# A two-layer kernel: one store per tile of values with its surroundings copied within DRAM, early loads moved behind C's rows, and attention's pools waiting tile by tile

## The chip, the cores and the metric

The kernel runs on one core of a Trainium2 chip. The core has five engines that work side by side, each through its own list of instructions in order: TensorE (PE), VectorE (DVE), ScalarE (ACT), GpSimd (POOL) and SyncE (SP), which here issues nearly all DMAs. The metric is the device time of the core in microseconds (us), the median of three runs. Engines wait for each other through semaphores; an instruction that waits holds back all that stands behind it on its engine, the issuing of DMAs included.

## The reference, cut to what matters

Input x is 4 images of 384 channels and 64 x 64 points. Each of two layers normalises x by groups and adds its output to x.

```python
# layer 0: a selective state-space layer over the L = 4096 points of an image
xz = einsum('blc,dc->bld', layernorm(gn(x)), in_proj_w)      # 384 -> 2 x 768
xb, z = split(xz)
xc = silu(causal_conv4(xb) + conv_b)
dt, B, C = split(xc @ x_proj_w.T)                             # 24, 16, 16
dt = softplus(dt @ dt_w.T + dt_b)
h_t = exp(dt_t * A) * h_{t-1} + (dt_t * xc_t) * B_t           # 768 x 16 states, along L
y = (sum over states of h_t * C_t + xc * D) * silu(z)
x = x + y @ out_proj_w.T
# layer 1: attention of each point over a window of 7 x 7 around it, 12 heads of 32
q, k, v = split(w_qkv @ gn(x));  k, v padded by 3 at each side with their edge values
attn = softmax(q * scale . k in the window + rel_bias)
x = x + w_proj @ (sum over the window of attn * v) + b_proj
```

Everything is float32. The change concerns the padded v, which both parts of the kernel hand to each other through DRAM.

## The kernel before, in words

**State-space layer** (`state_space_layer`, from line 366). The points of the four images are cut into 44 chunks of 372 or 376, eleven per image. A chunk is worked in 24 steps: 6 blocks of 128 channels by 4 groups of 4 states. For each step the drive dt*x*B is made by POOL or DVE (`drive`, line 908; the list `DRIVES`, line 109, says which), DVE runs four scans, POOL multiplies the states by C (`times_c`, line 952), PE sums them by transposing into a PSUM bank (`sums`, 966). B and C come as rows out of DRAM, spread over 128 partitions (`load_bc`, 781), eight buffers of 744 KB for both together. Ahead of the scans a chunk needs its projections: `load_w` (691) brings twelve pieces of the input projection's weights in turn into three buffers, `in_proj` (695) multiplies, `x_proj` (762) makes dt, B and C, and `x_rows` (772) copies them with ACT and stores B's and C's rows (bcrows).

All of this, for all chunks, is put into one list with a tick each (`put`, line 507; the ticks stand in the table `AT`, line 43, 16 ticks to a step, 384 to a chunk), sorted once by tick (line 1178) and written down in that order. `Written` (line 144) makes the instructions of each engine keep the written order. All instructions are made inside one helper, so the profile shows all of them as line 154. SP's list is thus the order of ticks too: a DMA that waits holds back the DMAs with later ticks, though SP runs ahead of the engines where nothing makes it wait. Each DMA signals one of eight semaphores in turn, and it is not issued before the DMA that used that semaphore last has landed.

From chunk 13 on, the layer also prepares attention for images already done: three tiles of 128 points per chunk of values (`value_load`, `value_mm`, `value_out`, `value_store`; the three stores have ticks 631, 263 and 458, that is 247 in the next chunk, 263, and 74 in the next chunk), and a tile of keys and one of queries. 88 tiles of values, 22 of the 32 stripes of attention, are made here. A tile k covers rows 2k and 2k+1 of the image.

`store_values` (line 323) writes a tile into `vdr`, the padded array of 70 x 70 points. It issues one DMA of 64 x 384 elements for each row, and for each side one of 3 x 384 that repeats the row's first or last point: six DMAs. The tile with an image's first or last row writes that row four times: fifteen DMAs. At tick 263 of one chunk comes the last tile of image 0 or 1, at tick 247 the first tile of image 0, 1 or 2; the third image's last rows are made in attention. Right behind the store at 247 (-137 seen from the next chunk) stands the load of a piece of w_in at tick -128, for the `in_proj` at -122.

**The hand-over.** `begin_attention` (line 1145) stands one tick after the last `in_proj`. It closes the pool of the projections' buffers, makes stripe 0's keys `kt`, queries `q` and the table `bias` in their place, and issues their six loads at once. In SP's list this is ahead of the last chunk's loads of B's last rows (tick 20) and of C's rows (21, 22, 62).

**Attention** (`attention_layer`, line 1181). 32 stripes of eight image rows; a stripe is 12 units (4 pairs of blocks of 8 x 8 points by 3 groups of 4 heads). The loop at line 1457 writes in each iteration parts of several units: `divide` (DVE, POOL), `scores` (PE, then DVE adds bias and takes the maximum, ACT the exponential), `turn` (PE transposes), `weigh` (PE, with the values `vw`), and projections for stripes ahead (`pieces`, 1350). `load_pair_values` (357) loads values of a pair as four DMAs of 98 x 384; `load_keys` (1272) loads keys and queries of a stripe. While the iteration number is negative these are issued by ACT, later by SP. `surround` (1277) copies a stripe's border keys between neighbours on POOL. Stripes 22 to 31 compute their values here (`value`, 1243), with the same `store_values`.

The attention pools are opened (line 1187) in the memory of the state-space layer's pools. Opened without `reuse_waits="tile"`, the first use of such memory waits for everything that used the old pools.

Of the kernel before, what the change touches and what calls it, by code (L numbers as in the profile page):

```python
# [15 lines left out]
C = 384  # L16
NJ = C // P
HW = 64
# [15 lines left out]
STEP = 16  # L34
CHUNK = STEP * STEPS
# [135 lines left out]
def two_layers(  # L171
# [150 lines left out]

    def store_values(dq, b, k, v):

        for row in range(2):
            y = 2 * k + row
            to = [PAD + y]
            if y == 0:
                to += range(PAD)
            if y == HW - 1:  # L330
                to += range(PAD + HW, HP)
            a = row * HW
            for t in to:
                dq.dma_start(vdr[b][t, PAD : PAD + HW, :], v[a : a + HW, :])
                for c, p in ((0, a), (PAD + HW, a + HW - 1)):
                    dq.dma_start(
                        vdr[b][t : t + 1, c : c + PAD, :],
                        v[p : p + 1, :].unsqueeze(1).broadcast_to([1, PAD, C]),
                    )

    def load_stripe_keys(dq, kt, s):
        b, r = s // NXT, s % NXT
        for m in range(NJ):
            dq.dma_start(
                kt[:, m, PAD : PAD + RB, PAD : PAD + HW],
                kdr[b][m * P : (m + 1) * P, r * TX : (r + 1) * TX].rearrange(
                    "p (r c) -> p r c", r=RB
                ),
            )

    def load_stripe_queries(dq, q, s):
        b, r = s // NXT, s % NXT
        dq.dma_start(
            q, qdr[b][:, r * TX : (r + 1) * TX].rearrange("(k p) t -> p k t", p=P)
        )
# [10 lines left out]
    def state_space_layer(eng):  # L366
# [5 lines left out]
        with ExitStack() as es:  # L372
# [134 lines left out]
            def put(tick, fn, *args):  # L507
                score.append((tick, len(score), fn, args))
# [588 lines left out]
                )  # L1097


            tiles = [(b, k) for b in range(NB - 1) for k in range(L // P)]  # L1100
            for X in range(len(chunks)):
                for i in range(len(AT["value_mm"])):
                    if not tiles or X < NCHUNK * (tiles[0][0] + 1) + 2:
                        break
                    b, k = tiles[0]
                    left = (len(chunks) - X) * len(AT["value_mm"]) - i
                    if k % NPAIR == 0 and left < NPAIR:
                        break
                    cell = {"at": tiles.pop(0)}
                    have_values.add((b, k))  # L1110
                    for name, fn in (
                        ("value_load", value_load), ("value_norm", value_norm),
                        ("value_mm", value_mm), ("value_out", value_out),
                        ("value_store", value_store),
                    ):
                        put(CHUNK * X + AT[name][i], fn, cell)


            turns = sorted(range(2 * NJ), key=lambda n: AT["key_mm"][n])
# [25 lines left out]
            def begin_attention():  # L1145
                preps.close()
                home = ctx.enter_context(
                    tc.tile_pool(name="early", bufs=1, reuse_waits="tile", side="right")
                )
                kt = home.tile([P, NJ, RW, HP], F32, name="kt0")  # L1150
                q = home.tile([P, NJ, TX], F32, name="q0")
                bias = early["bias"] = home.tile([P, NH, NK], F32, name="bias")
                early["kt"], early["q"] = [kt], [q]
                load_stripe_keys(dq, kt, 0)
                load_stripe_queries(dq, q, 0)
                for e in range(2):
                    dq.dma_start(bias[e * QB : (e + 1) * QB].rearrange("p h k -> p (h k)"), bm)

            put(
                CHUNK * (len(chunks) - 1) + 1 + max(  # L1160
                    max(AT[name]) for name in ("in_proj", "in_bias", "conv", "x_rows", "dt_mm")
                ),
                begin_attention,
            )


            put(-120, dq.dma_start, w_out, out_wT.rearrange("(k p) m -> p k m", p=P))
# [13 lines left out]
    def attention_layer(eng, gm1, qkb, pjb, early, mv):  # L1181
# [2 lines left out]
        stripes = NB * NXT  # L1184
        with ExitStack() as es:
            def pool(name, **kw):
                return es.enter_context(tc.tile_pool(name=name, **kw))

            wt = pool("wt1", bufs=1)
            w_qkv = wt.tile([P, NJ, 3 * C], F32, name="w_qkv")  # L1190
# [21 lines left out]
            def of(s):  # L1212
                return s // NXT, s % NXT
# [5 lines left out]
            def kt_of(s):  # L1219
                return ring([P, NJ, RW, HP], "kt", 4, s)  # L1220
# [7 lines left out]
            def vw_of(k):  # L1228
                return ring([P, 2, NCH, C], "vw", 3, k)
# [39 lines left out]
                )  # L1269
                surround(s, m)  # L1270

            def load_keys(s, dq):
                if s > 0:
                    load_stripe_keys(dq, kt_of(s), s)
                    load_stripe_queries(dq, q_of(s), s)

            def surround(s, m):

                b, r = of(s)
                kt = kt_of(s)  # L1280
                own = kt[:, m, PAD : PAD + RB, :]
                for c, e in ((0, PAD), (PAD + HW, PAD + HW - 1)):
                    ge.tensor_copy(
                        own[:, :, c : c + PAD], own[:, :, e : e + 1].broadcast_to([P, RB, PAD])
                    )
                if r > 0:
                    ge.tensor_copy(kt_of(s - 1)[:, m, PAD + RB :, :], own[:, 0:PAD, :])
                else:
                    ge.tensor_copy(kt[:, m, 0:PAD, :], own[:, 0:1, :].broadcast_to([P, PAD, HP]))
                if r < NXT - 1:  # L1290
                    ge.tensor_copy(kt_of(s + 1)[:, m, 0:PAD, :], own[:, RB - PAD :, :])
                else:
                    ge.tensor_copy(
                        kt[:, m, PAD + RB :, :], own[:, RB - 1 : RB, :].broadcast_to([P, PAD, HP])
                    )
# [46 lines left out]
            def has_values(s):  # L1342
                b, r = of(s)
                return (b, NPAIR * r) in have_values

            def has_keys(s):
                b, r = of(s)
                return (b, 2 * r) in have_keys and (b, 2 * r + 1) in have_keys
# [108 lines left out]
            for s in range(-3 * UNITS, N + 12):  # L1457
                stripe, k = s // UNITS, s % UNITS
                for f in waiting:
                    next(f, None)  # L1460
                waiting = []
                if s == 4:
                    output_bias(mm)
                if s > 4 and last_stats:
                    last_stats.pop(0)()
                if 0 <= s - 4 < N and (s - 4) % NJ == NJ - 1:
                    keep(s - 4)
                if 0 <= s - 1 < N:
                    divide(s - 1)
                if 0 <= s < N:  # L1470
                    scores(s)
                if 0 <= s - 2 < N:
                    turn(s - 2)
                mine = pieces(stripe, k)
                for n, (f, t, i) in enumerate(mine):
                    ps = mm if s >= 0 else (mm, *lgs)[(s + n) % 5]
                    if n == 1 and 0 <= s - 3 < N:
                        weigh(s - 3)
                    g = f(t, i, ps)
                    next(g)  # L1480
                    if n < len(mine) - 1:
                        next(g, None)
                    else:
                        waiting.append(g)
                if len(mine) < 2 and 0 <= s - 3 < N:
                    weigh(s - 3)
                if k == 0 and 0 <= stripe - 1 < stripes:
                    load_res(stripe - 1)
                if 0 <= stripe + 2 < stripes and has_keys(stripe + 2):
                    if k == 0:  # L1490
                        load_keys(stripe + 2, se if s < 0 else dq)
                    if k in (4, 6, 8):
                        surround(stripe + 2, (k - 4) // 2)
                if k == 2 and 0 <= stripe + 3 < stripes and not has_keys(stripe + 3):
                    load_x(stripe + 3)
                if s == 3 - UNITS:
                    dq.dma_start(w_pj, proj_wT.rearrange("(k p) m -> p k m", p=P))
                if s == 2 * UNITS:
                    dq.dma_start(w_qkv, qkv_wT.rearrange("(k p) m -> p k m", p=P))
                if 6 <= k < 6 + NJ and 0 <= stripe + 3 < stripes and not has_keys(stripe + 3):  # L1500
                    gn(stripe + 3, k - 6)
                pair = (s + 1) // NJ + 1
                if (s + 1) % NJ == 0 and 0 <= pair < stripes * NPAIR:
                    load_pair_values(se if s < 0 else dq, vw_of(pair), pair)

    engines = [
        Written(tc, e) for e in (nc.tensor, nc.vector, nc.scalar, nc.gpsimd, nc.sync)
# [49 lines left out]
```

## Time and profile before

| | us |
|---|---|
| median of three runs | 6690.64 (6688.14 to 6691.85) |
| the profiled execution's own time | 6691.2 |
| its span | 6689.4 |
| PE busy (matmul) in the span | 6224.9 |
| DVE, ACT, POOL busy | 5838.8, 5612.8, 5676.5 |
| last scan of the state-space layer ends | about 5158.5 |
| last statistics of the state-space layer end | 5182.2 |
| attention's first exponential starts | 5203.03 |

The page cuts the span into 40 slices of 167 us and gives each engine's busy tenths. A group row has the engine, the operation, output and inputs, the shapes, the number of instructions, then busy us and mean ns, then the idle time just ahead of the group and what ended most of it. In a timeline a row is a start, a duration, the instruction and how many of its kind follow one another; [5.91 <-ACT state] means that the engine had been idle for 5.91 us, and that an instruction of ACT on state ended that. SPq and ACTq rows are DMAs that SP or ACT issues, with the time its sequencer spent on them. A row of the windows view has a stretch, its length, then busy us and number of instructions of PE, PE's weight loads, DVE, ACT and POOL, the clock granted to PE, the mean busy share of the 16 DMA engines, and GB/s.

The time between two stores of bcrows is the length of a chunk. It is 112.6 us in chunks 38 to 42 and 113.5 in most of chunks 16 to 33; it is 119.28, 118.11, 120.52, 117.44 and 118.87 in the chunks that end at 1806, 2836, 3072, 4100 and 4335.

### The profile page before, as it was taken

Reading aid. Unit: us, or ns where it says so; the run is one execution under the profiler, and the core shown is the slowest. Engines: PE = TensorE matmul, PEld = TensorE weight load, DVE = VectorE, ACT = ScalarE, POOL = GpSimd, SP = SyncE. Lnnn points to the kernel's source line nnn. Section 1 sums busy time; section 2 is a strip of 40 time slices with the busy share of each in tenths; the row PEclk is TensorE's granted clock in tenths of the full one; section 3 lists DMA queues with packets and bytes.
Section 4 is the critical chain, followed back from the end, with each engine's and each line's share of the span. In section 5 each row is a group of like instructions: output and inputs, shape, how many; then the busy total and the mean of one; then the engine's idle time right before and its main releaser. Section 6 shows DMA issues by size and latency. Waiting matters only on the chain.

```text
span 6689.4 us, 134599 instructions
## 1 busy us (share of the span) xinstructions
PE 6224.9 (93%) x47526; PEld 4275.4 (64%) x47526; DVE 5838.8 (87%) x10102; ACT 5612.8 (84%) x14147; POOL 5676.5 (85%) x3032
## 2 busy tenths in 40 slices
PE   6888888989999999999999999999996899999999
PEld 4666666666666676666666666676765555555555
DVE  4999999999999999999999999999998666555555
ACT  4888888888999999999999999999995778665556
POOL 3999999999999999999999999999998555444443
PEclk9999999999999999999999999999998999999999
DMA  5242323232444445353535344453532555223332
GB/s 186 88 132 90 132 91 129 87 135 93 159 138 147 150 127 162 123 165 119 176 118 162 123 149 136 125 157 121 159 121 79 153 159 157 97 97 106 100 103 92
DMA packets 790234, 860.06 MB, mean 129 GB/s; under 512 B 200344, under 2 KB 710072, under 8 KB 789432
## 3 DMA queue, kind: packets, MB, share of 16 engines
q1 hardware_dynamic: 785200, 848.68, 40.2%
q8 instruction: 377, 6.18, 0.4%
q10 hardware_dynamic: 4360, 2.78, 0.2%
q14 instruction: 297, 2.43, 0.1%
HBM read 740.60 MB, written 110.81 MB: 127 GB/s over the span
## 4 chain that ended last, share of the span: by engine, by line
DVE 33%; PE 29%; ACT 26%; issue 6%; POOL 4%; DMA 1%; SPq 1%; POOLq 0%; DVEq 0%; ACTq 0%
DVE h L154 29%; PE mm L154 17%; ACT da L154 9%; PE pt L154 4%; POOL h L154 4%; PE yps L154 4%; ACT L154 3%; ACT sg L154 3%; PE ov L154 2%; PE lg L154 2%; ACT dt L154 2%; ACT sz L154 2%; DVE xn L154 1%; ACT xD L154 1%; ACT pT L154 1%
## 5 line engine op out<-in xcount | busy, mean ns | idle before, releaser
L154 DVE TENSOR_TENSOR_SCAN h<-da,h 128x373 f32<-128x373 f32 (+1 forms) x4224 | 3616.6, 913 | 88.4 <-ACT da L154 74.5
L154 POOL TENSOR_TENSOR h<-h,BC 128x1488 f32<-128x1488 f32 (+1 forms) x1056 | 3257.7, 3102 | 68.4 <-ACT state L154 65.2
L154 ACT ACTIVATE da<-dt,nega 128x372 f32<-128x372 f32 (+1 forms) x4224 | 2378.6, 571 | 313.7 <-DVE h L154 279.8
L154 POOL TENSOR_TENSOR h<-dtx,BC 128x372 f32<-128x372 f32 (+6 forms) x1056 | 1754.6, 1682 | 52.8 <-ACT dtx L154 35.8
L154 PE MATMUL yps<-ident,h 128*124 128x128 f32 (+1 forms) x12672 | 1603.7, 279 | 138.7 <-POOL h L154 136.7
L154 PEld LDWEIGHTS yps<-ident,h 128*124 128x124 f32 (+1 forms) x12672 | 1457.0, 142 | 352.5 <-POOL h L154 226.6
L154 PE MATMUL mm<-xn,w_in 128*128 128x372 f32 (+3 forms) x3168 | 1099.0, 487 | 84.0 <-DMA w_in<-wdr 40.5
L154 POOL TENSOR_TENSOR sg<-sg,rs 128x784 f32<-128x784 f32 x384 | 574.0, 1495 | 643.2 <-DVE rs L154 490.2
L154 ACT ACTIVATE sg<-sg,mx 128x196 f32<-128x196 f32 x1536 | 685.1, 448 | 404.6 <-DVE mx L154 359.7
L154 DVE TENSOR_TENSOR h<-dtxps,BC 128x1488 f32<-128x1488 f32 (+6 forms) x792 | 967.6, 1235 | 2.1 <-ACT dtx L154 1.4
L154 PEld LDWEIGHTS mm<-xn,w_in 128*128 128x128 f32 x3168 | 576.6, 192 | 417.6 <-DVE h L154 56.6
L154 PE MATMUL mm<-xb,cw 128*128 128x372 f32 (+1 forms) x2112 | 699.5, 477 | 23.9 <-ACT xc L154 18.2
L154 DVE CUSTOM_DVE_ANT_0 sg<-lg,bias 128x196 f32<-128x196 f32 x1536 | 464.3, 358 | 186.0 <-PE lg L154 177.9
L154 PEld LDWEIGHTS mm<-xb,cw 128*128 128x128 f32 x2112 | 393.8, 189 | 285.3 <-ACT xc L154 35.5
L154 ACT ACT_TABLE_LOAD x441 | 565.8, 1283 | 8.7 <-PEq L1542 0.8
L154 PE MATMUL mm<-yg,w_out 128*128 128x372 f32 (+1 forms) x1584 | 526.1, 478 | 0.0
L154 PE MATMUL pt<-ident,sg 128*98 128x128 f32 x3072 | 446.6, 281 | 29.0 <-ACT pT L154 21.4
L154 PEld LDWEIGHTS pt<-ident,sg 128*98 128x98 f32 x3072 | 313.7, 128 | 181.6 <-issue 78.7
L154 PEld LDWEIGHTS mm<-yg,w_out 128*128 128x128 f32 x1584 | 288.7, 191 | 152.9 <-issue 1.6
L154 PEld LDWEIGHTS ov<-pT,vw 98*32 98x32 f32 x12288 | 189.6, 110 | 193.3 <-issue 136.7
L154 ACT ACTIVATION_READ_ACCUMULATOR sg<-sg,mx 128x1 f32 x1536 | 287.8, 187 | 0.0
L154 PE MATMUL mm<-xp,w_qkv 128*128 128x512 f32 x612 | 279.5, 593 | 0.0
(136 smaller groups left out, 7106.3 us busy)
## 6 DMA issues: line engine op xcount, KB each, us to landing
BC<-bcrows SPq DMA_DIRECT2D x320, 744.0 KB
w_in<-wdr SPq DMA_DIRECT2D x528, 192.0 KB
vw<-vdr SPq DMA_DIRECT2D x504, 147.0 KB
cw<-ddr SPq DMA_DIRECT2D x264, 256.0 KB
xs<-in_x_dram SPq DMA_DIRECT2D x210, 186.0 KB
wk<-in_qkv_wT_dram SPq DMA_DIRECT2D x180, 192.0 KB
o<-x SPq DMA_DIRECT2D x96, 256.0 KB
out_dram<-o SPq DMA_DIRECT2D x96, 256.0 KB
```

Source lines behind the costliest of these rows:

```text
L154: ins = made(*args, **kw)
```

## The change

- A tile of values is stored by one DMA of 2 x 64 x 384 elements. The surroundings are made by a new function, `pad_values`, once per stripe: for each side one DMA from `vdr` to `vdr` that repeats the first or last column of eight rows three times, and for the first and last stripe of an image one that repeats a whole row of 70 points three times. In the state-space layer these stand 24, 48 and 72 ticks after the stripe's last store; in attention at units 6, 7 and 8 of the stripe two ahead of use.
- `begin_attention` stands behind the last C row (tick 62) too. Its loads follow one by one, 32 ticks apart: kt, q, and bias in two halves.
- All pools of attention are opened with `reuse_waits="tile"`: a tile waits for the last users of the tiles that lay in its memory.
- Before attention's first unit, ACT issues only the three loads of keys of stripe 1; that stripe's queries and the first two pairs of values are issued by SP.

PE's, DVE's and POOL's lists are otherwise the same instructions in the same order; ACT's lacks nine DMAs; SP's has 2633 rows in place of 3001.

```diff
     def store_values(dq, b, k, v):
-        for row in range(2):
-            y = 2 * k + row
-            to = [PAD + y]
-            if y == 0:
-                to += range(PAD)
-            if y == HW - 1:
-                to += range(PAD + HW, HP)
-            a = row * HW
-            for t in to:
-                dq.dma_start(vdr[b][t, PAD : PAD + HW, :], v[a : a + HW, :])
-                for c, p in ((0, a), (PAD + HW, a + HW - 1)):
-                    dq.dma_start(
-                        vdr[b][t : t + 1, c : c + PAD, :],
-                        v[p : p + 1, :].unsqueeze(1).broadcast_to([1, PAD, C]),
-                    )
+        dq.dma_start(vdr[b][PAD + 2 * k : PAD + 2 * k + 2, PAD : PAD + HW, :], v)
+
+    def pad_values(dq, b, r, side):
+        rows = vdr[b][PAD + RB * r : PAD + RB * (r + 1)]
+        if side < 2:
+            c, e = ((0, PAD), (PAD + HW, PAD + HW - 1))[side]
+            dq.dma_start(
+                rows[:, c : c + PAD, :], rows[:, e : e + 1, :].broadcast_to([RB, PAD, C])
+            )
+        elif r in (0, NXT - 1):
+            y, e = (0, PAD) if r == 0 else (PAD + HW, PAD + HW - 1)
+            dq.dma_start(
+                vdr[b][y : y + PAD], vdr[b][e : e + 1].broadcast_to([PAD, HP, C])
+            )
...
+                    stored[b, k // NPAIR] = max(
+                        stored.get((b, k // NPAIR), 0), CHUNK * X + AT["value_store"][i]
+                    )
+            for (b, r), tick in stored.items():
+                for side in range(3):
+                    put(tick + 24 * (side + 1), pad_values, dq, b, r, side)
...
                 early["kt"], early["q"] = [kt], [q]
-                load_stripe_keys(dq, kt, 0)
-                load_stripe_queries(dq, q, 0)
-                for e in range(2):
-                    dq.dma_start(bias[e * QB : (e + 1) * QB].rearrange("p h k -> p (h k)"), bm)
...
+            tick = CHUNK * (len(chunks) - 1) + 1 + max(
+                max(AT[name])
+                for name in ("in_proj", "in_bias", "conv", "x_rows", "dt_mm", "load_c")
+            )
+            put(tick, begin_attention)
+            for n in range(4):
+                put(tick + 2 * STEP * (n + 1), early_load, n)
...
-                return es.enter_context(tc.tile_pool(name=name, **kw))
+                return es.enter_context(tc.tile_pool(name=name, reuse_waits="tile", **kw))
...
-            def load_keys(s, dq):
+            def load_keys(s, key_queue):
                 if s > 0:
-                    load_stripe_keys(dq, kt_of(s), s)
+                    load_stripe_keys(key_queue, kt_of(s), s)
                     load_stripe_queries(dq, q_of(s), s)
...
+                t = stripe + 2
+                if 0 <= t < stripes and not has_values(t) and k in (6, 7, 8):
+                    pad_values(dq, *of(t), k - 6)
...
-                    load_pair_values(se if s < 0 else dq, vw_of(pair), pair)
+                    load_pair_values(dq, vw_of(pair), pair)
```

More of the change, by code (lines that the diff above doesn't have):

```diff
@@ L1097, in state_space_layer @@
                 )
+            stored = {}
             tiles = [(b, k) for b in range(NB - 1) for k in range(L // P)]
@@ L1153, in begin_attention, with early_load @@
                 early["kt"], early["q"] = [kt], [q]
-                load_stripe_keys(dq, kt, 0)
-                load_stripe_queries(dq, q, 0)
-                for e in range(2):
-                    dq.dma_start(bias[e * QB : (e + 1) * QB].rearrange("p h k -> p (h k)"), bm)
[L1159 to L1163, printed above, removed]
-            )
+            def early_load(n):
+                if n == 0:
+                    load_stripe_keys(dq, early["kt"][0], 0)
+                elif n == 1:
+                    load_stripe_queries(dq, early["q"][0], 0)
+                else:
+                    e = n - 2
+                    dq.dma_start(
+                        early["bias"][e * QB : (e + 1) * QB].rearrange("p h k -> p (h k)"), bm
+                    )
+            tick = CHUNK * (len(chunks) - 1) + 1 + max(
+                max(AT[name])
+                for name in ("in_proj", "in_bias", "conv", "x_rows", "dt_mm", "load_c")
+            )
+            put(tick, begin_attention)
+            for n in range(4):
+                put(tick + 2 * STEP * (n + 1), early_load, n)
             put(-120, dq.dma_start, w_out, out_wT.rearrange("(k p) m -> p k m", p=P))
```

## The prediction

> **What bounds the kernel now.** I read the page's engine shares and slices first, then the groups, then the timelines of POOL, SP, PE and ACT around every place where POOL idles. Slices 1 to 30 are the state-space layer, in which the slice rows give four engines 8 to 9 tenths; the rest is attention, in which PE alone has 9.
>
> ```profile
> PE   6888888989999999999999999999996899999999
> POOL 3999999999999999999999999999998555444443
> L154 POOL TENSOR_TENSOR h<-h,BC 128x1488 f32<-128x1488 f32 (+1 forms) x1056 | 3257.7, 3102 | 68.4 <-ACT state L154 65.2
> L154 POOL TENSOR_TENSOR h<-dtx,BC 128x372 f32<-128x372 f32 (+6 forms) x1056 | 1754.6, 1682 | 52.8 <-ACT dtx L154 35.8
> ```
>
> The two POOL groups make (3257.7 + 1754.6)/44 = 113.9 us of work per chunk, and bcrows issues follow one another by 112.6 to 113.5 us in most chunks: POOL sets the pace, and an interval longer than that is one in which POOL idled. Its timeline shows where. The first case, SP beside PE and POOL, in the chunk that stores the first tile of image 0:
>
> ```profile
> 1786.41 9.33 SPq L154 DMA_DIRECT2D vdr<-vo  x15
> 1795.79 0.41 SPq L154 DMA_DIRECT2D w_in<-wdr  x1
> ...
> 1798.37 3.51 PE L154 MATMUL mm<-xn,w_in 128*128 128x372 f32 x6 [6.51 <-DVE h L154]
> ...
> 1806.40 3.09 POOL L154 TENSOR_TENSOR h<-h,BC 128x1488 f32<-128x1488 f32 x1 [5.91 <-ACT state L154]
> ```
>
> Fifteen value DMAs hold SP for 9.33 us; w_in is issued behind them, PE starts 2.6 us after that issue, and ACT, in order behind PE's x_proj, releases POOL 5.91 us late. An ordinary chunk has six DMAs there:
>
> ```profile
> 4884.96 3.74 SPq L154 DMA_DIRECT2D vdr<-vo  x6
> 4888.74 0.41 SPq L154 DMA_DIRECT2D w_in<-wdr  x1
> ...
> 4891.29 2.11 PE L154 MATMUL mm<-xn,w_in 128*128 128x372 f32 x6 [0.89 <-DMA w_in<-wdr]
> 4893.24 3.91 PE L154 MATMUL mm<-xc,w_xp 128*128 128x372 f32 x12
> ...
> 4898.45 0.46 ACT L154 COPY xd<-mm 128x372 f32<-128x372 f32 x1
> ```
>
> PE waits 0.89 us, but x_proj ends at 4897.15 and ACT takes it at 4898.45: 1.3 us of cover, and POOL does not idle. The second place is the last chunk, the third the hand-over to attention:
>
> ```profile
> 5037.97 2.20 SPq L154 DMA_DIRECT2D kt<-kdr  x3
> 5042.48 4.95 SPq L154 DMA_DIRECT2D BC<-bcrows  x4
> ...
> 5055.16 3.49 POOL L154 TENSOR_TENSOR h<-dtx,BC 128x752 f32<-128x752 f32 x2 [8.07 <-DMA BC<-bcrows]
> ...
> 5182.39 3.25 ACTq L154 DMA_DIRECT2D kt<-kdr  x3
> 5188.20 14.78 ACTq L154 DMA_DIRECT2D vw<-vdr  x8
> 5203.03 0.46 ACT L154 ACTIVATE sg<-sg,mx 128x196 f32<-128x196 f32 x1 [36.17 <-DMA vw<-vdr]
> ```
>
> SP waits from 5031.8 to 5037.97 for PE to free kt's memory, with B's last rows and C's rows queued behind it. At the hand-over ACT's sequencer issues twelve loads from 5182.39 to 5202.98 while everything else waits for its first exponential.
>
> **What the Trainium skill says.** DMA: Bandwidth & Descriptors, section "Why a DMA increments its semaphore by 16 and not by 1": a DMA from SP or ACT uses k engines, the largest k up to 16 that divides the slowest dimension on both sides. A stretch with nothing but vw loads (98 partitions from 7 rows, so k = 7) agrees, with a DMA share of 0.44 = 7/16:
>
> ```profile
> 6117.50:6119.00 1.50, 1.50 (x5) 0.57 (x3) 0.35 (x1) 1.28 (x5) 1.39 (x2) 1.00 0.44 164
> ```
>
> So the new store, two rows from 128 partitions, should use 2 engines where the old 64x384 used 16. Same page, "Queues, rings and completion order": on each engine SP's DMAs are consumed in order, so what is issued after such a store waits on those two engines; no view of before isolates that. Same page, "Two DMAs through the same engine are not ordered": the copies within DRAM must wait for the store's semaphore; the built program has that wait on SP.
>
> **The change part by part**, against the profiled execution (6691.2 us, span 6689.4; the median, 6690.64, is 0.6 less).
>
> (a) *Stores.* A tile's DMAs fall from 6 (15 at an image's first and last row) to 1. In ordinary chunks SP is free 3 us earlier per store, which is worth nothing where POOL has no idle. At the five edge tiles (stores x15 at 1786, 2824, 3051, 4088, 4315) POOL's idle goes: 5.91 + 1.63 + 7.17 + 2.54 + 6.39 = 23.6, and the idles in the next half chunk are longer than usual by 0.85 + 0.35 + 0.87 + 0.5 + 0.4 = 3.0. Sum 26.6 us. What is late next there is the ordinary 0.89 us, covered.
>
> New cost: the store's 64 descriptors on each of two engines. The window above gives 164/(0.44 x 16) = 23.3 GB/s per engine, 66 ns for 1536 B; a window over one old 64x384 store has share 0.81 at 191 GB/s, 14.7 GB/s, 104 ns, but that is four descriptors per engine, start included. Bounds 4.2 and 6.7 us. Windows show its data starting at about 4886.4. At 66 ns w_in follows on those engines: 4886.4 + 4.2 + eight of its own, 0.5, + 0.64 (end of data to PE's start, as now) = 4891.8, 0.5 us later than now: inside the 1.3. At 104 ns it is 2.9 later. I take 66, the rate of a long stream, and nothing lost; queued behind SP's issue in that place are w_in, wk and bcrows.
>
> (b) *Copies.* Two per stripe (three at edges), 22 stripes in the state-space layer. Side copies are 24 descriptors on k = 8: under 1 us. SP's wait for the last store falls where SP now waits for vo or xd anyway (next issues at 4890.94 and 4898.94). The copies of whole rows have k = 3, two 53,760 B descriptors per engine: 4.6 us at 23.3 GB/s (7.3 at 14.7) on three engines, ahead of w_in and B's rows, which have some 3 to 5 us of slack. Cost over five edges between 0 and 15 us; I take 2.
>
> (c) *Early loads.* kt, q and bias move past the last B and C rows, the value store and q's stores, so SP does not stand at 5031.8. B's last load waits then for POOL's multiplication ending near 5034.5; one chunk earlier it was issued at 4922.89, which puts it at 5035.5, and with 6 us to landing (the chain has BC at 5.97 and 6.25) it is there at 5042, before POOL wants it at 5047.1. The 8.07 us go. After 5055 POOL has no idle until 5164.7, so it stays the bound; DVE, which idled 10.9 us in that stretch, isn't late next. The moved loads land near 5095, needed at 5170: hidden by 75 us of POOL. Gain 8.1; bounds 6 and 9.
>
> (d) *Attention's pools, and who issues.* In the built program kt's three ACT loads no longer wait for the last residual, statistics and store: the first can go after ACT's last yt (5166.9), the third after the first residual's store has landed (about 5174.5). The nine others go to SP. So PE's scores follow out_proj (5178.8), DVE's first reduction follows the statistics (ends 5182.2, against 5190.23 now), and ACT's exponential starts at 5182.6 in place of 5203.03: 20.4 us. Next late: vw for the first weighting, 8.4 us after the first exponential now, so due at 5191. SP issues q, w_pj, then vw from 5179.8 on: 768 + 576 KB at 373 GB/s (16 x 23.3) from 5181.5, then 588 KB at 164 GB/s, makes 5189, plus 1 us to the semaphore. kt of stripe 2 is due at 5195.6 and follows at about 5195. Both just fit; I take 20.0, bounds 15 and 22.
>
> (e) *Attention's own stores and copies*: PE waits under 9 us in all after 6000 us, none of it for a DMA, and vw, which queues on SP behind the side copies' wait, is loaded seven units ahead: 0, bounds -2 and +5. DVE reuses a v buffer after three units, some 11 us, over the store's 7.
>
> Sum: 26.6 + 0 - 2 + 8.1 + 20.0 = 52.7; 6691.2 - 52.7 = 6638.5, against the median 6638.
>
> **Rivals.**
> 1. *The two-engine store, slower than before.* At 104 ns each w_in is 2.9 us late, 1.6 beyond its cover, in each of 31 chunks with values, and with the edges' ratio of total to direct idle (26.6/23.6): 31 x 1.6 x 1.13 = 56 us, 6694. It starts to cost at 79 ns (4886.4 + 64 x 0.079 + 1.14 is 1.3 after 4891.29) and passes the time before at 103; for it speaks the 104 of the short stores, against it the 66 of vw. Chance 0.05, half of it over 0.2%.
> 2. *Row copies block.* w_in or B's rows behind them arrive 3 us late at each edge: half of (a) lost, 6651. For: two long descriptors on three engines; against: they come after bcrows. 0.13.
> 3. *Hand-over only moves on.* vw or kt late: ACT starts at 5182.6 but weighting waits; 10 of the 20 lost, 6648. 0.12.
> 4. *C's rows don't do it*: POOL late for another input, 8 lost, 6646. 0.05.
>
> **How the numbers follow.** The forecast has 0.65: 6638, itself 6629 to 6646. Low end: (b) at nothing, (d) at 22, (c) at 9, (e) at -2, and some us of PE clock, which is 0.74 in 5150 to 5200 and suffers from idleness: 6629. High end takes in rivals 2 to 4 and (a) at 84 ns (0.4 us beyond cover, 13 us in all): 6660. A difference under 0.2%, 13 us, is about what cannot be told from none. Faster by more: 0.65 + 0.13 + 0.12 + 0.05 less a little, 0.94; same 0.03; slower 0.03.
>
> **What would show it.** Right: no POOL idle over 1 us at the five edges; no idle before B's rows in the last chunk; ACT's first exponential near 5150 (5203.03 - 52.7). Wrong: PE's wait for w_in grown from 0.9 to over 2 us per chunk and a chunk interval over 113.5 (rival 1); waits behind row copies; PE or POOL waiting for vw or kt in attention's first 20 us; attention itself longer than 1486 us from its first exponential.

## The result and the profile after

The changed kernel takes 6638.8 us, the median of six runs (6638.07 to 6644.35), against 6689.1 us for the kernel before (six runs, 6687.83 to 6691.85). The ratio is 0.9926, with a 95% interval from 0.9913 to 0.9939. Its profiled execution has a span of 6636.4 us, 53.0 less than the span before.

In the groups of the page after, POOL's two in the state-space layer are:

```profile
L154 POOL TENSOR_TENSOR h<-h,BC 128x1488 f32<-128x1488 f32 (+1 forms) x1056 | 3259.8, 3104 | 45.0 <-ACT state L154 41.5
L154 POOL TENSOR_TENSOR h<-dtx,BC 128x372 f32<-128x372 f32 (+6 forms) x1056 | 1756.2, 1684 | 42.7 <-ACT dtx L154 34.1
```

POOL's work is the same; what shrank is its idle time, 68.4 to 45.0 and 52.8 to 42.7 us. SP issues 3167 DMAs in this trace, where it issued 3798 before: 128 tiles had 840 DMAs and have 128 and 72 copies now, and nine came over from ACT. (The 2633 and 3001 rows given above are not these counts.) At the place of the first edge, image 0's first tile, POOL now runs through. This is a timeline of the changed kernel, SP beside PE and POOL:

```profile
1784.00 0.52 SPq L154 DMA_DIRECT2D vdr<-vo  x1
1784.56 0.47 SPq L154 DMA_DIRECT2D w_in<-wdr  x1
...
1790.95 2.12 PE L154 MATMUL mm<-xn,w_in 128*128 128x372 f32 x6 [1.50 <-DMA w_in<-wdr]
...
1794.08 3.09 POOL L154 TENSOR_TENSOR h<-h,BC 128x1488 f32<-128x1488 f32 x1
```

One store of 0.52 us stands where fifteen held SP for 9.33, and the idle of 5.91 us ahead of POOL's multiplication is gone. But w_in, issued 0.56 us after the store, now keeps PE waiting 1.50 us. It does so, or a little longer, in nearly every chunk from here on, and the ordinary chunks (113.5 or 112.6 us before) are a little longer: 113.8 and 112.9 us. The last chunk and the hand-over in the changed kernel:

```profile
5005.90 15.98 SPq L154 DMA_DIRECT2D BC<-bcrows  x5
5021.44 3.56 POOL L154 TENSOR_TENSOR h<-dtx,BC 128x752 f32<-128x752 f32 x2
...
5033.19 2.05 SPq L154 DMA_DIRECT2D kt<-kdr  x3
...
5148.80 0.46 ACT L154 ACTIVATE sg<-sg,mx 128x196 f32<-128x196 f32 x1 [15.56 <-DVE mx L154]
```

B's and C's rows stand ahead of kt, and POOL's multiplication with B's last rows, which had waited 8.07 us, starts without idle at 5021.44. ACT's first exponential now waits for DVE's maximum, not for its own queue of loads. It starts at 5148.80, where it was 5203.03.

The stages can be told apart by three marks: the store of bcrows of a chunk, the start of PE's last row of sums of states (5164.76 before, 5131.13 after), and the first exponential. From the store of bcrows of chunk 12 to that of chunk 43 the change gains 23.3 us (3554.35 to 3531.07), from there to the last sum 8.0, from the last sum to the first exponential 20.6 (38.27 to 17.67). Attention takes 1487.6 us from there, 1.2 more. The other 2.4 us of the 53.0 were there before any changed instruction, so they are not the change's: up to chunk 12 the lists of all kernels below are the same, and that store comes between 1452.5 and 1455.9 us in their profiles.

### The profile page after: what moved, and what is told of

It reads as the page before. It is cut to its first block, busy times and chain, and to the rows that moved or that the text cites. A ratio compares the mean times of both kernels' runs of the same rounds, so it can differ in the third digit from the quotient of the medians.

```text
span 6636.4 us, 133738 instructions
## 1 busy us (share of the span) xinstructions
PE 6220.8 (94%) x47526; PEld 4267.2 (64%) x47526; DVE 5838.6 (88%) x10102; ACT 5612.0 (85%) x14147; POOL 5679.2 (86%) x3032
## 4 chain that ended last, share of the span: by engine, by line
DVE 32%; PE 32%; ACT 25%; issue 5%; POOL 4%; DMA 2%; SPq 0%; POOLq 0%; DVEq 0%; ACTq 0%
DVE h L154 28%; PE mm L154 19%; ACT da L154 8%; PE yps L154 5%; PE pt L154 4%; POOL h L154 3%; ACT sg L154 3%; ACT L154 3%; PE ov L154 2%; PE lg L154 2%; ACT dt L154 2%; ACT sz L154 2%; DVE xn L154 1%; DMA w_in<-wdr 1%; ACT pT L154 1%
## 5 line engine op out<-in xcount | busy, mean ns | idle before, releaser
L154 POOL TENSOR_TENSOR h<-dtx,BC 128x372 f32<-128x372 f32 (+6 forms) x1056 | 1756.2, 1684 | 42.7 <-ACT dtx L154 34.1
```

Source lines behind the costliest of these rows:

```text
L154: ins = made(*args, **kw)
```

## The experiments

The theory after the result: the change has three gains that add up, and one loss which the prediction put at nothing, the two-engine store. The rivals are named with each run. Ratios are to the kernel before, with 95% intervals.

**One part at a time.** The first run has the kernel before with the new `store_values` and `pad_values`, the second with the early loads behind C's rows, the third with

```diff
-                return es.enter_context(tc.tile_pool(name=name, **kw))
+                return es.enter_context(tc.tile_pool(name=name, reuse_waits="tile", **kw))
...
-                    load_pair_values(se if s < 0 else dq, vw_of(pair), pair)
+                    load_pair_values(dq, vw_of(pair), pair)
```

and the same for the first queries.

> The kernel before with one part of the change: one store per tile and the surroundings copied within DRAM; early loads, pools and ACT's loads stay as before. Theory: the five edge chunks lose their long POOL idles (-25.6 us by the two traces), but the store on two engines makes w_in about 0.6 us later in every chunk with values, PE's x_proj and dt_mm follow 0.6 us later, and ACT, which waits there with only 0.37 us to spare, slips 0.25 to 0.33 us per chunk, +7 to +8 us over 26 ordinary chunks: about 6671 us against 6689.1, ordinary chunks of 113.8 and 112.9 us. Prediction on record for this part alone: 24.6 us less, 6664.5. Rival (the longer ordinary chunks come from the other parts or from run to run): chunks of 113.5 and 112.6 us and 6663 us.

> The kernel before with one part of the change: stripe 0's keys, queries and bias are loaded behind the last C rows, one by one. Theory and prediction: 8 us less (6681 us), POOL's 8.07 us idle before B's last rows gone, ordinary and edge chunks exactly as before (113.5, 112.6). Rival: what comes behind it at the hand-over gives some of it back, 6684 to 6689 us.

> The kernel before with one part of the change: attention's pools wait tile by tile, and SP issues the first pairs of values and queries. Theory: ACT's first exponential comes 20 us earlier in relation to the last step of the state-space layer, 6669 us; chunks as before. Rival (the two parts at the end overlap, because SP in front of the hand-over is held up by kt's early loads): 12 to 15 us, 6675 us.

Measured: 6667.9 us (0.9966, 0.9952 to 0.9979), 6680.0 (0.9986, 0.9980 to 0.9993), 6669.4 (0.9970, 0.9959 to 0.9981). Against 6689.2 these are 21.3, 9.2 and 19.9 us, together 50.4; the whole change has 50.3. That these agree to 0.1 is chance, since the parts' intervals are 9 to 18 us wide, but the stages in the traces say the same: 23.9, 8.0 and 20.6 us alone, 23.3, 8.0 and 20.6 in the whole. So the parts do not overlap, against the third run's rival. The first run's ordinary chunks are 113.7 to 113.9 and 112.8 to 113.1 us; the second's and third's are 113.5 and 112.6. The loss per chunk belongs to the stores. In the second run the last sum follows the store of chunk 43 by 8.0 us less than before; in the third the first exponential comes 17.66 us after the last sum.

**What in the store costs.** Two edits of the changed kernel, the first with two DMAs per tile, the second with only a store's place moved (the copies that follow a stripe's last store move with it):

```diff
-        dq.dma_start(vdr[b][PAD + 2 * k : PAD + 2 * k + 2, PAD : PAD + HW, :], v)
+        for row in range(2):
+            dq.dma_start(
+                vdr[b][PAD + 2 * k + row, PAD : PAD + HW, :], v[row * HW : (row + 1) * HW, :]
+            )
```

```diff
-    value_store=(631, 263, 458),
+    value_store=(641, 263, 458),
```

> The changed kernel with a tile's store cut into two DMAs of 64 x 384 (one per image row), all else as changed. Theory (the store's two engines delay w_in): w_in's wait on PE is back at 0.9 us from 1.5, ordinary chunks are back at 113.5 and 112.6 us, the edge chunks keep their gain: 7 to 9 us less than the changed kernel, 6630 to 6632 us. Rival (the copies within DRAM or the changed order of SP's list make the chunks longer): 6638 to 6640 us, chunks of 113.8 and 112.9.

> The changed kernel with only the place of one store moved: its tick 631 becomes 641, so that it stands behind the load of w_in at tick -128 of the next chunk, and not ahead of it. It is still one DMA of 2 x 64 x 384. Theory (it is what stands behind the two-engine store that is late, and only w_in is close to its end): ordinary chunks of 113.5 and 112.6 us as with two DMAs, 6630 to 6634 us. Rival (a store on two engines costs wherever it stands, because other loads share its engines): 6637 to 6640 us, chunks of 113.8 and 112.9 us.

Measured: 6633.1 us (0.9917, 0.9904 to 0.9931) and 6632.5 us (0.9916, 0.9902 to 0.9929), the fastest two versions here. The intervals overlap with the change's own, but the chunks decide: with two DMAs the ordinary ones are 113.50 and 112.60 us again, to the hundredth as before; with the moved store 113.57 and 112.67. From chunk 12 to 43 that is 7.1 and 5.5 us less than the changed kernel. The copies within DRAM are the same in all three and SP's list nearly so, and the first run's rival falls. The second run's rival, a store on two engines that costs wherever it stands, keeps 0.07 of some 0.3 us per chunk. In neither run does PE wait for w_in at this place in an ordinary chunk; 0.9 us was expected in the first. That the chunks are still no shorter than before shows that the 0.89 us of the kernel before were covered.

Where 0.25 to 0.3 us per chunk come from is read in three timelines of the same place, PE's `dt_mm` (w_dt) beside ACT. Before:

```profile
4899.70 0.90 PE L154 MATMUL mm<-xd,w_dt 24*128 24x372 f32 x6
4899.71 1.28 ACT L154 ACT_TABLE_LOAD   x1
...
4901.00 1.50 ACT L154 ACTIVATE dt<-mm,dtb 128x372 f32<-128x372 f32 x3
```

The changed kernel, w_in's wait included:

```profile
4866.13 2.12 PE L154 MATMUL mm<-xn,w_in 128*128 128x372 f32 x6 [1.50 <-DMA w_in<-wdr]
...
4872.68 0.46 ACT L154 COPY xd<-mm 128x372 f32<-128x372 f32 x1
...
4873.94 1.28 ACT L154 ACT_TABLE_LOAD   x1
4874.55 0.90 PE L154 MATMUL mm<-xd,w_dt 24*128 24x372 f32 x6
...
4875.47 1.50 ACT L154 ACTIVATE dt<-mm,dtb 128x372 f32<-128x372 f32 x3 [0.25 <-PE mm L154]
```

With two DMAs:

```profile
4869.09 0.90 PE L154 MATMUL mm<-xd,w_dt 24*128 24x372 f32 x6
...
4869.84 1.28 ACT L154 ACT_TABLE_LOAD   x1
...
4871.14 1.49 ACT L154 ACTIVATE dt<-mm,dtb 128x372 f32<-128x372 f32 x3
```

Seen from ACT's copy of xd, which is on time in both (4898.45 before, 25.77 us after 4872.68), PE's w_in matmuls start 0.6 us later in the changed kernel, and `dt_mm` too. ACT takes `dt_mm`'s result 0.92 us after its start in the changed kernel. Before, that result was there at 4900.62, and ACT, busy with a table load, came at 4901.00: 0.38 us of cover. Of 0.62 us, 0.24 is left over, and ACT shows it as its 0.25. The next to wait is DVE's scan. The chain that ended last (start, us, what), and DVE, in the changed kernel:

```profile
4859.74 6.25 DMA w_in<-wdr
...
4878.89 3.41 DVE L154 TENSOR_TENSOR_SCAN h<-da,h 128x373 f32<-128x373 f32 x4 [0.22 <-ACT da L154]
```

From the load of w_in the chain goes on through PE and ACT. Before, at this place it goes from DVE's scans to ACT, with neither w_in nor PE on it, and the scan starts without idle. In an ordinary chunk (2034.03 to 2147.53 before, 2025.52 to 2139.30 after) DVE's idle grows from 0.75 to 1.00 us, and the chunk from 113.50 to 113.78.

**Doubling the store.** Three tries on the changed kernel. The first writes each tile twice to its place. The second writes it first to a contiguous piece of DRAM that nothing reads, the third to such a piece with rows 70 points apart (the third's edit is shown):

```diff
+        dq.dma_start(vscr[k % 2][:, PAD : PAD + HW, :], v)
         dq.dma_start(vdr[b][PAD + 2 * k : PAD + 2 * k + 2, PAD : PAD + HW, :], v)
```

> The changed kernel with each tile's store issued twice, the same data to the same place. Theory: the second store puts 64 more descriptors on the same two engines ahead of w_in, some 4.2 us at 66 ns each; w_in is then about 4.8 us later than before, all beyond the 0.37 us that ACT has to spare, and each chunk with values is 3.5 to 4.5 us longer than with one store: ordinary chunks of about 117.5 us, 31 x 4 = 124 us more, some 6760 us. If the wait per descriptor is 104 ns, it is 6.7 us per chunk and 6840 us. Rival (the w_in load does not queue behind the store's data, and its 0.6 us come from SP): 1 to 10 us more, 6640 to 6650 us.

> The changed kernel with a second store of each tile, of the same form and from the same buffer, ahead of the real one and into memory that nothing reads (two such pieces in turn), so that SP does not wait for the first store to land as it did in the run that stored twice to one place (SP stood 6.8 us per pair there). Only the data on the store's two engines is doubled. Theory: 64 more descriptors of 65 ns (4.2 us) ahead of w_in, none of it covered: ordinary chunks of 113.8 + 4.2 = 118.0 us and 112.9 + 4.2 = 117.1 us, 31 x 4.2 = 130 us more, 6769 us. Rival (w_in does not queue behind the store's data): under 10 us more, 6645 us.

> The changed kernel with an extra store of each tile ahead of the real one, as in the run before, but with the rows of the unread piece 70 points apart, as in the padded array. In that run the piece was one contiguous block, and the extra store went over all 16 engines. Theory: now it uses two, 64 descriptors of 65 ns each ahead of w_in, which comes 4.2 us later; and PE, having stood for 5 us or so, works off in_proj and x_proj at a lower clock, some 2 us more by the two runs before: ordinary chunks of 119 to 120 us (113.8 + 4.2 + 2), 31 x 6 = 186 us more, about 6825 us. Without the clock's part: 118 us, 6769 us. Rival (the store's data does not delay w_in, only SP and the 16 engines did in the run before): as in the run before, 6702 us or less.

The first gave 6986.7 us (1.0443, 1.0429 to 1.0457), far beyond what was expected, with ordinary chunks of 121 to 123 us. Its timeline shows why, SP and PE:

```profile
4979.45 6.83 SPq L154 DMA_DIRECT2D vdr<-vo  x2
...
4986.33 0.47 SPq L154 DMA_DIRECT2D w_in<-wdr  x1
...
4992.94 4.06 PE L154 MATMUL mm<-xn,w_in 128*128 128x372 f32 x6 [8.02 <-DMA w_in<-wdr]
```

The second store to the same place is not issued before the first has landed, so the pair holds SP 6.83 us, and all behind it. That is another wait than the one in question, and the run does not decide it.

The second gave 6702.1 us (1.0019, 1.0012 to 1.0026), less than the theory's 6769 and more than the rival's 6645. Two windows of its trace:

```profile
4919.00:4920.00 1.00, 1.00 (x8) 0.64 (x7) 1.00 (x2) 0.98 (x2) 1.00 (x2) 1.00 0.89 290
4921.50:4924.50 3.00, 2.01 (x7) 0.92 (x6) 3.00 (x4) 2.68 (x6) 3.00 (x3) 1.00 0.13 41
```

The DMA share is 0.89 in the first, and falls to 0.13, two of 16 engines, for 3 us: no more than one store leaves. The extra store went over many engines; what sets it apart from the real one is that its piece was contiguous. w_in came 1.3 us later (PE waits 2.80 in place of 1.50), and the ordinary chunks are 114.0 to 116.7 us.

The third differs only in the distance of the rows and gave 6820.2 us (1.0194, 1.0177 to 1.0211; 6825 expected). Its ordinary chunks are 119.5 us in place of 113.8. PE waits 5.59 us for w_in, 4.1 more. The rest is the clock, in two windows on PE's wait and the matmuls behind it:

```profile
5033.20:5038.70 5.50, 0.00 (x0) 0.00 (x0) 5.50 (x7) 4.59 (x12) 5.50 (x4) 0.85 0.13 50
5038.80:5042.80 4.00, 4.00 (x7) 2.28 (x8) 0.90 (x2) 0.00 (x0) 3.00 (x2) 0.50 0.43 137
```

While PE waits, the share is 0.13 at 50 GB/s: w_in stands behind two stores' data. Then PE runs at 0.50 of its clock, and six matmuls take 4.06 us, not 2.12. 4.1 + 1.9 is 6.0, and 5.7 were measured. So rival 1's mechanism is real: 1.3 us more of delay for w_in already made the kernel slower than the one before, by 0.2%, and 4.1 us more by 1.9%. The 4.1 us are 64 ns for each of the extra store's 64 rows on an engine; with one store at that rate the change met only the mechanism's beginning.

**Whether the edges were SP's list or the number of DMAs.** The kernel before, with the tick 631 alone changed to 641:

> The kernel before with six or fifteen DMAs per tile as ever, but with the store of tick 631 at 641, behind the load of w_in. Theory (SP's list holds w_in up at the three edges whose fifteen DMAs stand ahead of it): the edges with idles of 5.91, 7.17 and 6.39 us fall to about what the two edges behind w_in cost (1.63 and 2.54, the loads of wk and bcrows behind them being late), 10 to 16 us less, 6673 to 6679 us; ordinary chunks as before. Rival (the number of DMAs costs, wherever they stand): no change, 6686 to 6690 us.

Measured: 6671.5 us (0.9973, 0.9963 to 0.9983). The three edges with the fifteen DMAs ahead of w_in are 115.22, 115.72 and 114.33 us, where they were 119.28, 120.52 and 118.87; the two behind w_in are as before (117.95 and 117.40, against 118.11 and 117.44). The number is the same 15, so most of its cost came from its place, and the rival falls. What is left, 1.7 to 2.2 us over an ordinary chunk at these three, goes only with fewer DMAs. Moving this one store gives 18.5 of the 50 us by the medians and 15.9 by the traces, chunk 12 to 43; 10 to 16 were expected.

**The hand-over in halves.** The kernel before with `reuse_waits="tile"` alone, and with SP's issuing alone:

> The kernel before with attention's pools waiting tile by tile, but with ACT still issuing all twelve loads ahead of the first unit. Theory: ACT issues its first loads some 8 to 10 us earlier (after its last yt and the first residual's store instead of after all that used the old memory), but the nine others still hold its sequencer for some 15 us: its first exponential comes about 9 us earlier than before in relation to the last step, 6680 us. Rival (the pools alone do it, and ACT's issuing is hidden behind the loads' own time): 20 us, 6669 us. Other rival (the values' buffers wait for late users of their memory all the same): 0 to 3 us, 6687 us.

> The kernel before with SP, not ACT, issuing the first values and queries of attention; its pools still wait for everything that used their memory. Theory: ACT's three loads of keys still start at 5182 and take 3.3 us, DVE's first reduction is done at 5190 as before, and the first exponential follows at 5190.5 in place of 5203: 12 us less, 6677 us; with the pools alone (4 us by the run before) that is 16 to 17 of the 20 us of both together. Rival (SP's loads wait as late as ACT's did, and the values come late for the first weighting): 3 to 6 us, 6684 us.

Measured: 6686.2 us (0.9995, 0.9986 to 1.0003) and 6681.8 us (0.9988, 0.9981 to 0.9994). The first can't be told from the kernel before by its time, and both gained less than expected. The timeline of the kernel with the pools alone, ACT and its queue:

```profile
5165.43 0.40 ACTq L154 DMA_DIRECT2D kt<-kdr  x1
...
5180.61 0.41 ACTq L154 DMA_DIRECT2D q<-qdr  x1
...
5181.14 16.31 ACTq L154 DMA_DIRECT2D vw<-vdr  x8
...
5197.56 0.46 ACT L154 ACTIVATE sg<-sg,mx 128x196 f32<-128x196 f32 x1 [31.64 <-DMA vw<-vdr]
```

Seen from the last sum, kt is issued 16 us earlier than before, but q, at 5180.61, only some 4 us earlier; ACT then issues eight vw loads until 5197.5, and the exponential stands behind them. So part of the second rival (late users of the memory hold the loads) is there too; what q waits for was not traced. With SP issuing alone:

```profile
5179.93 4.28 ACTq L154 DMA_DIRECT2D kt<-kdr  x3
...
5187.20 0.96 PE L154 MATMUL lg<-kt,q 32*64 32x196 f32 x16 [10.82 <-POOL kt L154]
...
5188.77 0.46 ACT L154 ACTIVATE sg<-sg,mx 128x196 f32<-128x196 f32 x1 [24.37 <-DVE mx L154]
...
5192.22 0.96 PE L154 MATMUL lg<-kt,q 32*64 32x196 f32 x16 [4.06 <-POOL kt L154]
```

kt is as late as ever, and PE's scores wait for it, by way of POOL, which copies its border points. From the last sum to the first exponential it is 38.27 us before, 33.76 with the pools, 26.47 with SP, 17.67 with both: 4.5 and 11.8, and 20.6 together. But with SP alone the next scores wait for POOL's kt too (4.06 us), and attention from the first exponential on is 3.2 us longer than before. In the medians the halves give 3.7 and 7.6 us and both 19.9: each half leaves the other's wait in place, and some 8 us come only with both.

## Why the prediction was right, point by point

- *(a) The edges*: 26.6 us were forecast from POOL's idles. With two DMAs per tile, where no loss is mixed in, the stage gains 30.4 us (3554.35 to 3523.97, chunk 12 to 43). The five edge chunks alone are 26.3 shorter, where the idles gave 23.6; the ones after them 3.7, where they gave 3.0. Adding up the idles that stood out missed 3.8. In the changed kernel POOL has no idle over 1 us at the places of the five idles, the sign that the prediction named.
- *What sets the pace*: the prediction has POOL, from (3257.7 + 1754.6)/44 = 113.9 us. This sum counts the overlapping ends of successive instructions twice and is longer than a chunk of 112.6 us. In the chunk 2034.03 to 2147.53 of the kernel before, of 113.50 us, DVE is busy for 112.75 and POOL for 112.37, and the chain that ended last is 49% DVE and 39% ACT there, with no POOL on it. POOL's long idles still marked the edges, because all three stood still there (at the first, ACT 5.17 us for PE's in_proj, DVE 4.63 and 1.62 for ACT, POOL 5.91 for ACT); how little slack ACT and DVE had for a small delay, they did not show.
- *(a) The two-engine store*: the mechanism and its size were right. The windows of the changed kernel have, in the last 3 us before PE's start, only two of 16 engines at work, on the store's rest and on w_in's rows behind it:

```profile
4862.50:4865.50 3.00, 2.13 (x8) 1.03 (x6) 3.00 (x4) 2.68 (x5) 3.00 (x3) 1.00 0.13 48
```

  w_in was to be 0.5 us later, and PE is 0.62 later behind it. PE's wait for it grew from 0.9 to 1.5 us, not to over 2, but the ordinary chunk did pass 113.5: rival 1's sign came in part. The step that failed is "inside the 1.3", with "nothing lost". The 1.3 us lay between x_proj and ACT's xd, but PE also carries the delay past xd to `dt_mm`, and there only 0.38 was to spare. Cost: 7.1 us from chunk 12 to 43, put at 0. The sentence on the Trainium skill (DMA: Bandwidth & Descriptors, "Why a DMA increments its semaphore by 16 and not by 1") holds: k follows from the slowest dimension "as the instruction carries it"; two rows 70 points apart were stored by two engines (a share of 0.13), the contiguous piece by more (0.89). No run shows how the instruction carries the contiguous piece. That w_in waits behind a store on its two engines, for which the prediction had no view, is shown by the third run of the doubling: 4.1 us for 64 more rows on each.
- *(b) The copies*: taken at 2 us, they cost nothing that shows: in the version with two DMAs the first and third edge chunks (images 0 and 1, first tile) are 113.50 and 113.49 us, and the chunks behind them 113.50 too, like all ordinary ones.
- *(c) C's rows*: 8.1 forecast, 8.0 measured, alone and in the whole.
- *(d) The hand-over*: 20.0 forecast (20.4 worked out, less something for what "just fits"), 20.6 measured. vw and kt are in time: PE's waits in the first 35 us of attention are for issue and ACT, none for a load.
- *(e) Attention's own stores*: 0 forecast. From the first exponential to the end the kernels with the old stores take 1486.3 to 1489.6 us, the changed one 1487.6: nothing that can be told from none, though over the 1486 that the prediction named as a sign.

The sum 52.7 stands against 53.0 in the spans, of which 2.4 are the start, and 50.3 in the medians; the terms that were missed, +3.8, -7.1 and +2, nearly cancel. So part of the closeness is luck: with the missed gains alone the forecast would have come out 5.8 us too high, with the missed loss alone 7.1 too low. Of the rivals, 2, 3 and 4 did not happen. Why the moved store still leaves 0.07 us per chunk stays open; it isn't PE's wait for w_in, which is gone there.

## What to carry to other kernels

A delay's cover is the smallest slack among all the instructions behind it on its engine, not the slack of the next one (here 0.38 us, not 1.3); follow it through the whole list to the engines that set the pace, and read these from a chunk's busy time and from the chain, not from a sum of means. A store's cost to a full schedule is what stands behind it, in the issuing engine's list and on the DMA engines that it uses: move it behind the critical load before making it cheaper (moving one store gave 18.5 us here). When two waits end at nearly the same time, take both away; alone they gave 3.7 and 7.6 us of 19.9.

## What the runs showed of the hardware that was not expected

- PE's clock. Behind a wait for w_in of 1.4 to 1.7 us, six matmuls took 2.11 to 2.13 us (26 cases in the changed kernel). Behind one of 2.4 to 2.9 us, in the run with the extra store in one piece, 19 of 26 took 2.9 to 4.1 us and seven took 2.1. Three waits of 3.0 to 3.1 us (C's rows alone, the pools alone, SP alone) still left it at 2.1; behind 3.2 us and more, in all kernels, they took 3.5 to 4.1, at a mean granted clock of 0.50 to 0.60. So the wait of 5.59 us above cost PE 7.5. The Trainium skill (TensorE: Matmul & The Clock Gate, "What's actually happening") has the drop to half after an idle window of about 3.4 us; shorter waits, of 2.4 to 2.9 us, were enough in most cases here. The edges of the kernel before contained it too: the 3.51 us of six matmuls behind 6.51 us of idle.
- In the run that stored twice to one place, a 192 KB store on two engines lands some 6.3 us after SP issues it (6.83 us for the pair, less about 0.5 for an issue). While only such stores move, 50 GB/s pass at a share of 0.13, that is 25 GB/s for each of two engines, close to the 23.3 that the prediction took.
